# Expert-choice feed-forward on one core: first output unit reordered, weight sums and list tables moved

## Chip, core and metric

The kernel runs on one core of one Trainium2 chip. The metric is the device time of one execution in microseconds (us). TensorE (PE) multiplies, VectorE (DVE) and ScalarE (ACT) do the elementwise work, GpSimd (POOL) and SyncE (SP) issue transfers. Each engine works through its own queue in order, and semaphores tie the queues together.

## What is computed

The reference, cut to what matters (8 x 512 tokens of 512 values, 8 experts, 1024 tokens for each, 2048 hidden values):

```python
y = clip(einsum('blc,oc->blo', x * styles, weight) * dcoefs + bias, -256, 256)
scores = softmax(y @ Wr)                      # over 8 experts
G, idx = top_k(scores.T, 1024)                # each expert takes its best tokens
h = gelu(einsum('ekd,edh->ekh', y[idx], W1) + b1)
X_e = einsum('ekh,ehd->ekd', h, W2) + b2
out = x + zeros.at[idx].add(G[..., None] * X_e)
```

## The kernel before, in words

All products are in fp32. A first part (to about 130 us) forms y and the scores, stores both in a table in device memory, and finds expert 0's token list: `route_first` gives the position of each token as two digits, `first_indices` (L909 to L942) turns the digits into one-hot tables `hot` (L918), `val` (L923, L924) and `oh` (L930), and 64 small products `ps_idx` give the list. Fillers (`idle`) keep TensorE going beside it. `first_tokens` then gathers the tokens.

The rest is 16 pairs of a hidden and an output stage: for each expert `e` two halves `p` of the hidden values. Each product of a stage is done as a 2 x 2 block product with seven products instead of eight: p1 = a11 b11, p2 = a12 b21, p3 = s4 b22, p4 = a22 t4, p5 = s1 t1, p6 = s2 t2, p7 = s3 t3. The s are sums of blocks of the left side (`left_sums`, L978 to L983, on VectorE, in the order s3, s1, s2, s4), the t sums of the weights' blocks. t1 and t3 of w2 are made by accumulating transfers that POOL issues (L205, L206); t2 and t4 are two additions on VectorE (L221, L222, 128x1024).

*Hidden stage* (`hidden_stage`): the seven products are split into seven again (`second_level`), and a written list `ORDER` says in which order all of them go; "2b6" is inner step 6 of outer product 2 for half b. At a letter "w" other work is put in: the list `work` that the caller hands over, by place 0 to 3. The place of w2's sums is U - 2 = 2, the third "w", between 2b2 and 1b1. Results leave the accumulation banks (PSUM) by ScalarE copies (L1129) and VectorE additions (L1138 after step 2, L1149 after 5, L1157 after 4), and `hidden_outputs` adds them up (L1196, L1212 to L1216) and applies gelu on ScalarE (L1197).

*Output stage*: four units `out_unit`, one for each 128 rows of both token halves. `in_turns` runs them: it takes the first five steps of a unit as its own and keeps the other two as `held`, which it runs inside the next unit, one after that unit's first step and one after its second. Unit v: p1, p2, p6, p7, p5, then p3 and p4 held. Steps p1, p6, p5, p3 add up in one bank of tag a, and ScalarE copies the partial sum (`snap_o`, L1328) between them; p2 has tag b (one bank), p7 and p4 share one of two banks of tag c. A finished half row goes out by an indirect transfer that adds to the result (`send`, L1361).

The scheduler of the language may move instructions within what the dependencies allow; the order it makes on each engine is part of the build, and a reader sees it in the trace. Tile tags with a fixed number of buffers (`bufs`) decide what waits for what.

Of the kernel before, what the change touches and what calls it, by code (L numbers as in the profile page):

```python
# [12 lines left out]
BF16 = mybir.dt.bfloat16  # L13
I32 = mybir.dt.int32
AF = mybir.ActivationFunctionType
ALU = mybir.AluOpType
# [4 lines left out]
P = 128  # L21
# [4 lines left out]
def tile_modulated_expert_choice_ffn(  # L26
# [15 lines left out]
    nc = tc.nc  # L42
    B, L, C = x.shape
    W = condT.shape[0]
    E, D, H = w1.shape
    N = B * L
    K = max(4, math.ceil(N * 2.0 / E))
    NT = N // P
# [4 lines left out]
    GH = HALF // P  # L53
# [5 lines left out]
    YW = D + E  # L59
# [8 lines left out]
    wpool = ctx.enter_context(tc.tile_pool(name="weights", bufs=1))  # L68
# [6 lines left out]
    behind = {}  # L75
# [18 lines left out]
    ps = ps_mm.tile([P, HALF], F32, tag="c", name="ps_idle0", bufs=2)  # L94
# [817 lines left out]
    def first_indices():  # L912


        lo, hi = places[0]
        hot = gp.tile([P, 2 * GH * YW], BF16, tag="xg", name="hot_0")[:, 0 : NT * HI].rearrange(
            "p (t h) -> p t h", h=HI)
        nc.vector.tensor_tensor(hot, hi.unsqueeze(2).to_broadcast([P, NT, HI]),  # L918
                                iota_hi.unsqueeze(1).to_broadcast([P, NT, HI]), ALU.is_equal)
        both = gp.tile([P, 2 * GH * YW], BF16, tag="xg", name="oh_0")  # L920
        val = both[:, 0 : 2 * NT * HI].rearrange("p (t a h) -> p t a h", a=2, h=HI)
        oh = both[:, 2 * NT * HI : 2 * NT * HI + NT * LO].rearrange("p (t m) -> p t m", m=LO)
        nc.scalar.mul(val[:, :, 0, :], hot, iota_p[:, 0:1])  # L923
        nc.vector.tensor_tensor(val[:, :, 1, :], hot,  # L924
                                iota_t.unsqueeze(2).to_broadcast([P, NT, HI]), ALU.mult)
        parts = 4
        ps = ps_small.tile([P, 2, KG], F32, tag="small", name="ps_idx0")
        for n in range(parts):
            here = slice(n * NT // parts, (n + 1) * NT // parts)
            nc.vector.tensor_tensor(  # L930
                oh[:, here, :], lo[:, here].unsqueeze(2).to_broadcast([P, NT // parts, LO]),
                iota_lo[:, 0:LO].unsqueeze(1).to_broadcast([P, NT // parts, LO]), ALU.is_equal)
            for t in range(NT)[here]:
                for q in range(P // LO):
                    in_order(partial(
                        nc.tensor.matmul, ps[q * LO : (q + 1) * LO, :, :], oh[:, t, :],
                        val[:, t, :, :].rearrange("p a (g q) -> p q a g", q=P // LO)[:, q, :, :],
                        start=(t == 0), stop=(t == NT - 1), skip_group_check=True))
        idle(IDLE2, ps_mm.tile([P, HALF], F32, tag="b", name="ps_idle2"))
        idx_f = rt2.tile([P, KG], F32, tag="idx_f", name="idx_f_0")  # L940
        nc.vector.tensor_reduce(idx_f, ps.rearrange("p a k -> p k a"), AX.X, ALU.add)
        nc.vector.tensor_copy(idx[:, 0, :], idx_f)  # L942
# [120 lines left out]
    def bank(tag, name, bufs):  # L1063
        return ps_mm.tile([P, HALF], F32, tag=tag, name=f"ps_{tag}_{name}", bufs=bufs)

    def in_turns(units, between, keep=False, behind={}):

        held = []
        nxt = units[0]()
        for n in range(len(units)):
            unit = nxt
            if n + 1 < len(units):
                nxt = units[n + 1]()
            first = unit[:5]
            first[0]()
            if held:
                held[0]()  # L1080
            mark = first[1]()
            if held:
                held[1]()
            for f in first[2:]:
                mark = f() or mark
            for work in between.get(n, ()):
                with tc.issue_after(behind.get("last", mark).ins):
                    work()
            held = unit[5:]
        if keep:  # L1090
            return held
        for f in held:
            f()
# [211 lines left out]
    def out_unit(e, p, v, H, b2_sb):  # L1305

        _, gain, ngain = tokens[e]
        blk = w2_blocks[e, p]
        name = f"o{e}_{p}_{v}"
        c = v * P  # L1310
        a = {(i, k): H[:, :, k, i * HALF + c : i * HALF + c + P] for i in range(2) for k in range(2)}
        s = {n: sp.tile([P, HALF], F32, tag=f"snap{t}", name=f"h{n}_{name}").rearrange(
            "p (k m) -> p k m", m=P) for n, t in (("s2", 1), ("s3", 2), ("s4", 4))}
        s["s1"] = a[1, 0]
        with tc.issue_after(summed["last"].ins) if v == 1 else ExitStack():
            summed["last"] = left_sums(a[0, 0], a[0, 1], a[1, 0], a[1, 1], s)
        s["11"], s["12"], s["22"] = a[0, 0], a[0, 1], a[1, 1]
        G = [(gain[:, g : g + 1], ngain[:, g : g + 1]) for g in (v, v + GH)]
        o = [op.tile([P, D], F32, tag=f"o{i}", name=f"o{i}_{name}", bufs=2 + i) for i in range(2)]
        st = {}  # L1320

        def mm(ps, left, right, start):
            product(ps, [s[left][:, k, :] for k in range(U)],
                    [blk[right][:, k, :] for k in range(U)], start)

        def snap(n, scale):
            t = sp.tile([P, QD], F32, tag=f"osnap{n}", name=f"snap{n}_{name}", bufs=SNAPS[n])
            nc.scalar.mul(t, st["a"], scale)  # L1328
            return t

        def p1():
            st["a"] = bank("a", name, 2)[:, 0:QD]
            mm(st["a"], "11", (0, 0), True)
            st["s1"] = snap(1, G[0][0])

        def p2():
            b = bank("b", name, 1)[:, 0:QD]
            mm(b, "12", (1, 0), True)
            return nc.vector.scalar_tensor_tensor(o[0][:, 0:QD], b, G[0][0], st["s1"],
                                                  op0=ALU.mult, op1=ALU.add)  # L1340

        def p6():
            mm(st["a"], "s2", "t2", False)
            st["u2"] = snap(2, G[1][0])

        def p7():
            st["c"] = bank("c", name, 2)[:, 0:QD]
            mm(st["c"], "s3", "t3", True)

        def p5():  # L1350
            mm(st["a"], "s1", "t1", False)
            st["u4"] = snap(4, G[1][1])
            nc.vector.scalar_tensor_tensor(o[1][:, QD:D], st["c"], G[1][1], st["u4"],
                                           op0=ALU.mult, op1=ALU.add)

        def send(i):
            if p == 0:
                nc.vector.scalar_tensor_tensor(o[i], b2_sb, G[i][0], o[i],  # L1358
                                               op0=ALU.mult, op1=ALU.add)
            g = i * GH + v  # L1360
            sent["last"] = nc.gpsimd.indirect_dma_start(  # L1361
                out=last_rows[g] if e == E - 1 else out_rows,
                out_offset=bass.IndirectOffsetOnAxis(ap=idx[:, e, g : g + 1], axis=0),
                in_=o[i][:, :], in_offset=None, compute_op=ALU.add,
            )

        def p3():
            mm(st["a"], "s4", (1, 1), False)
            nc.scalar.mul(o[0][:, QD:D], st["a"], G[0][1])
            send(0)  # L1370

        def p4():
            mm(st["c"], "22", "t4", False)
            nc.vector.scalar_tensor_tensor(o[1][:, 0:QD], st["c"], G[1][0], st["u2"],
                                           op0=ALU.mult, op1=ALU.add)
            send(1)

        def last_p7():
            p7()
            nc.vector.scalar_tensor_tensor(o[1][:, 0:QD], st["c"], G[1][0], st["u2"],  # L1380
                                           op0=ALU.mult, op1=ALU.add)

        def last_p4():
            b = bank("b", name + "_p4", 1)[:, 0:QD]
            mm(b, "22", "t4", True)
            nc.vector.scalar_tensor_tensor(o[1][:, 0:QD], b, G[1][0], o[1][:, 0:QD],  # L1386
                                           op0=ALU.mult, op1=ALU.add)
            send(1)

        if (e, p, v) == (E - 1, NP - 1, GH - 1):  # L1390
            return [p1, p2, p6, last_p7, p5, last_p4, p3]
        return [p1, p2, p6, p7, p5, p3, p4]
# [16 lines left out]
    for e in range(E):  # L1409
# [3 lines left out]
        for p in range(NP):  # L1413
            nxt = (e, p + 1) if p + 1 < NP else (e + 1, 0)
            if e or p:
                H = fx.tile([P, U, 2, KG * P], F32, tag="H", name=f"H_{e}_{p}")
            work = {U - 2: [partial(sums, "w2", w2_blocks, (e, p))]}
            if e == p == 0:
                work[0] = [route_others]
            if p == NP - 1 and e + 1 < E:  # L1420
# [15 lines left out]
            if e == p == 0:  # L1436
                work[0] = [partial(second_sums, 0)]
            held = in_turns([partial(out_unit, e, p, v, H, b2_sb) for v in range(GH)], work,
                            keep=nxt[0] < E, behind=summed)


# [38 lines left out]
```

## Time and profile before

| what | value |
|---|---|
| median of 3 runs | 1663.96 us (1662.77 to 1664.11) |
| profiled execution | 1666.56 us, its span 1664.8 us |
| mean granted TensorE clock | 0.995 |
| hidden stage, expert 0 second half (273 to 325 us) | TensorE busy 52.0, VectorE 44.6, ScalarE 31.3 us |
| output stage, expert 0 second half (325 to 364 us) | TensorE busy 39.0, VectorE 38.8, ScalarE 6.2 us |
| sums of w2, L221 and L222 | 16 of each, median 1219 and 1218 ns |

A line of the timeline gives the start in us from the span's start, the length, the engine, the line of the kernel, the operation, what is written and read, the shape and the number of instructions merged; in brackets is the idle time before it and who ended it. A 128x256 matmul in fp32 is recorded as two instructions ("x8" is one product of a unit). The ends of matmuls are modelled, so two in a row overlap in the records, and only their starts tell of a short pause.

### The profile page before, as it was taken

How to read it: one execution, taken by the hardware profiler on the slowest of the kernel's cores; microseconds unless marked ns; L12 is line 12 of the kernel's file. 1: busy time of each engine (PE TensorE's matmuls, PEld its weight loads, DVE VectorE, ACT ScalarE, POOL GpSimd, SP SyncE). 2: the span in 40 equal slices, each digit the busy share in tenths (PEclk: the TensorE clock that was granted, in tenths of full speed). 3: DMA queues.
4: the chain of work that ended last, by engine and by line, in shares of the span. 5: the costliest groups of instructions: out<-in, count | busy, mean ns of one | idle time of the engine just before them, and what ended most of it. 6: DMA issues, size and time to landing. Idle time of an engine off the chain costs nothing. (4 is left out here: it accounts for less than half of the span.)

```text
span 1664.8 us, 22093 instructions
## 1 busy us (share of the span) xinstructions
PE 1637.1 (98%) x8001; PEld 1376.2 (83%) x8001; DVE 1309.3 (79%) x2392; ACT 665.0 (40%) x1505; POOL 432.7 (26%) x296
## 2 busy tenths in 40 slices
PE   9998999999999999999999999999999999999998
PEld 5785568888888888888888888888888888888887
DVE  5885699888879786978789686978689786977681
ACT  3543322516152533525161534435261625344351
POOL 0111004231342214230434224230423134331302
PEclk9999999999999999999999999999999999999999
DMA  9724716872686546963686557873686358774604
GB/s 210 187 52 151 237 51 126 211 155 49 128 207 149 120 102 140 238 122 79 116 190 151 95 108 165 210 133 85 120 202 151 59 125 187 171 133 102 127 1 51
DMA packets 178461, 224.51 MB, mean 135 GB/s; under 512 B 18216, under 2 KB 117288, under 8 KB 178224
## 3 DMA queue, kind: packets, MB, share of 16 engines
q0 software_dynamic: 48368, 92.69, 32.8%
q1 hardware_dynamic: 129968, 130.40, 27.9%
q8 instruction: 63, 1.03, 0.3%
q14 instruction: 46, 0.38, 0.1%
q10 hardware_dynamic: 16, 0.02, 0.0%
HBM read 166.07 MB, written 65.37 MB: 139 GB/s over the span
## 5 line engine op out<-in xcount | busy, mean ns | idle before, releaser
L1361 POOL DMA_INDIRECT out<-o_o,idx x128 | 265.5, 2074 | 601.2 <-DVE o_o L1358 80.6
L1129 ACT ACTIVATE q<-ps_qa 128x256 f32<-128x256 f32 x450 | 168.9, 383 | 145.9 <-PE ps_qa L1098 101.2
L1328 ACT ACTIVATE snap_o<-ps_a_o,gain 128x256 f32<-128x256 f32 x128 | 60.5, 473 | 337.6 <-PE ps_a_o L1098 337.6
L1196 DVE TENSOR_TENSOR H<-H,q 128x512 f32<-128x512 f32 x240 | 159.9, 687 | 22.2 <-ACT H L1153 12.0
L1197 ACT ACTIVATE H<-H,b_sb 128x512 f32<-128x512 f32 x240 | 166.1, 717 | 27.1 <-DVE H L1196 23.9
L1098 PE MATMUL ps_c_qc<-x_sums,w_l 128*128 128x256 f32 x420 | 126.6, 383 | 1.4 <-DVE H L1157 1.4
L1098 PE MATMUL ps_a_o<-w,H 128*128 128x256 f32 x512 | 127.0, 380 | 0.0
L1098 PE MATMUL ps_c_qc<-x_l,w_sums 128*128 128x256 f32 x420 | 125.1, 379 | 0.9 <-DVE H L1149 0.9
L1098 PE MATMUL ps_c_o<-w,hs_o 128*128 128x256 f32 x512 | 125.3, 382 | 0.0
L1098 PE MATMUL ps_b_qb<-x_l,w_l 128*128 128x256 f32 x420 | 125.0, 379 | 0.0
L1098 PE MATMUL ps_b_o<-w,H 128*128 128x256 f32 x512 | 123.7, 379 | 0.0
L1098 PE MATMUL ps_a_o<-w_t,hs_o 128*128 128x256 f32 x512 | 122.3, 381 | 0.0
L1098 PE MATMUL ps_a_o<-w,hs_o 128*128 128x256 f32 x512 | 121.2, 379 | 0.0
L1098 PE MATMUL ps_a_o<-w_t,H 128*128 128x256 f32 x512 | 121.2, 379 | 0.0
L206 POOL DMA_DIRECT2D w_l<-in_w x14 | 18.4, 1313 | 388.8 <-DMA w_l<-in_w 207.8
L1098 PE MATMUL ps_c_o<-w_t,H 128*128 128x256 f32 x504 | 119.1, 379 | 0.0
L1098 PEld LDWEIGHTS ps_c_o<-w,hs_o 128*128 128x128 f32 x512 | 95.9, 190 | 18.3 <-DVE hs_o L980 5.4
L1098 PEld LDWEIGHTS ps_a_o<-w_t,hs_o 128*128 128x128 f32 x512 | 96.0, 190 | 15.9 <-issue 3.4
L1098 PEld LDWEIGHTS ps_a_o<-w_t,H 128*128 128x128 f32 x512 | 96.4, 190 | 14.4 <-issue 0.5
L1098 PEld LDWEIGHTS ps_a_o<-w,H 128*128 128x128 f32 x512 | 96.6, 190 | 13.9 <-issue 1.1
L1098 PEld LDWEIGHTS ps_b_o<-w,H 128*128 128x128 f32 x512 | 97.1, 190 | 13.2
L1098 PEld LDWEIGHTS ps_a_o<-w,hs_o 128*128 128x128 f32 x512 | 95.6, 190 | 14.8
(326 smaller groups left out, 3289.2 us busy)
## 6 DMA issues: line engine op xcount, KB each, us to landing
w_l<-in_w SPq DMA_DIRECT2D x70, 512.0 KB
w<-in_w SPq DMA_DIRECT2D x64, 512.0 KB
rows<-xg SPq DMA_DIRECT2D x56, 260.0 KB
xg<-rows SPq DMA_DIRECT2D x56, 256.0 KB
w_l<-in_w POOLq DMA_DIRECT2D x28, 512.0 KB
w_t<-in_w SPq DMA_DIRECT2D x15, 512.0 KB
w<-in_w POOLq DMA_DIRECT2D x15, 512.0 KB
w_t<-in_w POOLq DMA_DIRECT2D x15, 512.0 KB
```

The source lines that it names most:

```text
L206: nc.gpsimd.dma_start(out=out[0, 1], in_=where[1, 1], accum_op=ALU.add)
L1098: nc.tensor.matmul(ps, lefts[k], rights[k], start=(start and k == 0), stop=(k == n - 1), skip_group_check=True)
L1129: nc.scalar.mul(t, st["a"], scale)
L1196: nc.vector.tensor_add(out[i, j], out[i, j], st[n])
L1197: nc.scalar.activation(out[i, j], out[i, j], AF.Gelu, bias=bias[j], scale=scale)
L1328: nc.scalar.mul(t, st["a"], scale)
L1361: sent["last"] = nc.gpsimd.indirect_dma_start(out=last_rows[g] if e == E - 1 else out_rows, out_offset=bass.IndirectOffsetOnAxis(ap=idx[:, ...
```

## The change

Three edits.

1. In each output stage the unit v = 0 gets another list of steps: p1, p2, p4, p7, p6, p5, p3, where p4 has a bank of tag c of its own, ScalarE copies its product to the output row, and the other parts are added to that row as they come. The list of five own steps so ends with p6, and p5 and p3 are held. `in_turns` gets `ahead`: the second unit's p1 is then run right after the first unit's p4.
2. The sums of w2 go to place U - 1 = 3, the fourth "w", between 6b2 and 5b1, in all stages but expert 0's first half.
3. `hot`, `val` and `oh` of `first_indices` lie in the tiles `w2_t2` and `w2_t4` of the weights' pool instead of the gather pool's tag "xg".

```diff
-        hot = gp.tile([P, 2 * GH * YW], BF16, tag="xg", name="hot_0")[:, 0 : NT * HI].rearrange(
-            "p (t h) -> p t h", h=HI)
+        room, oh = [wpool.tile([P, 2 * U * QD], BF16, tag=f"w2_t{n}", name=f"digits_{n}")
+                    for n in (2, 4)]
+        hot = room[:, 0 : NT * HI].rearrange("p (t h) -> p t h", h=HI)
...
-        both = gp.tile([P, 2 * GH * YW], BF16, tag="xg", name="oh_0")
-        val = both[:, 0 : 2 * NT * HI].rearrange("p (t a h) -> p t a h", a=2, h=HI)
-        oh = both[:, 2 * NT * HI : 2 * NT * HI + NT * LO].rearrange("p (t m) -> p t m", m=LO)
+        val = room[:, NT * HI : 3 * NT * HI].rearrange("p (t a h) -> p t a h", a=2, h=HI)
+        oh = oh[:, 0 : NT * LO].rearrange("p (t m) -> p t m", m=LO)
...
-    def in_turns(units, between, keep=False, behind={}):
+    def in_turns(units, between, keep=False, behind={}, ahead=False):
...
             first = unit[:5]
-            first[0]()
+            if not begun:
+                first[0]()
+            begun = False
...
-            for f in first[2:]:
+            for k, f in enumerate(first[2:]):
                 mark = f() or mark
+                if ahead and n == k == 0:
+                    nxt[0]()
+                    begun = True
...
+        def first_p4():
+            ps = bank("c", name + "_p4", 2)[:, 0:QD]
+            mm(ps, "22", "t4", True)
+            nc.scalar.mul(o[1][:, 0:QD], ps, G[1][0])
+        def first_p7():
+            p7()
+            nc.vector.scalar_tensor_tensor(o[1][:, 0:QD], st["c"], G[1][0], o[1][:, 0:QD],
+                                           op0=ALU.mult, op1=ALU.add)
+        def first_p6():
+            p6()
+            nc.vector.tensor_add(o[1][:, 0:QD], o[1][:, 0:QD], st["u2"])
+        def first_p5():
+            p5()
+            send(1)
+        if v == 0:
+            return [p1, p2, first_p4, first_p7, first_p6, first_p5, p3]
...
-            work = {U - 2: [partial(sums, "w2", w2_blocks, (e, p))]}
+            work = {(U - 1 if e or p else U - 2): [partial(sums, "w2", w2_blocks, (e, p))]}
...
-                            keep=nxt[0] < E, behind=summed)
+                            keep=nxt[0] < E, behind=summed, ahead=True)
```

## Prediction

> **What bounds the kernel now.** I read the page first, then who TensorE waits for, then the order in time of single stages. The page says that TensorE is busy nearly throughout (at a mean granted clock of 0.995):
>
> ```profile
> PE 1637.1 (98%) x8001; PEld 1376.2 (83%) x8001; DVE 1309.3 (79%) x2392; ACT 665.0 (40%) x1505; POOL 432.7 (26%) x296
> ```
>
> So only TensorE's pauses can be won. The list of waits names few (line, releaser, total, times, longest):
>
> ```profile
> PE ps_idx L81 <- DVE oh L924: 3.9, 1, 3.9
> ...
> PE ps_c_qc L1098 <- DVE H L1157: 1.4, 2, 0.8
> ```
>
> It hides pauses shorter than a matmul's modelled tail, so I compare starts. Eight 128x256 matmuls in a row start 1.73 us after the last eight: 0.216 us each. Where an output stage begins (expert 1, first half):
>
> ```profile
> 415.64 1.46 PE L1098 MATMUL ps_a_o<-w,H 128*128 128x256 f32 x6
> 417.03 1.56 PE L1098 MATMUL ps_c_o<-w,hs_o 128*128 128x256 f32 x6
> 418.45 1.97 PE L1098 MATMUL ps_a_o<-w_t,hs_o 128*128 128x256 f32 x8
> 420.26 0.59 PE L1098 MATMUL ps_c_o<-w,hs_o 128*128 128x256 f32 x2
> ```
>
> From 415.64 to 420.26 are 4.62 us for 20 matmuls, which need 4.32: 0.30 us are lost, because `hs_o` comes late from VectorE:
>
> ```profile
> 416.30 0.68 DVE L980 TENSOR_TENSOR hs_o<-H 128x512 f32<-128x512 f32 x1
> 417.01 0.69 DVE L981 TENSOR_TENSOR H<-H 128x512 f32<-128x512 f32 x1
> 417.62 0.68 DVE L982 SCALAR_TENSOR_TENSOR hs_o<-hs_o,H 128x512 f32<-128x512 f32 x1
> ```
>
> The second pause lies in the hidden stage before, where the two sums of w2 stand ahead of L1157, which frees a bank of tag c:
>
> ```profile
> 392.46 1.22 DVE L221 TENSOR_TENSOR w_t<-w_t,w 128x1024 f32<-128x1024 f32 x1
> 393.60 0.42 DVE L1149 TENSOR_TENSOR H<-q,ps_c_qc 128x256 f32<-128x256 f32 x1
> 393.94 1.22 DVE L222 TENSOR_TENSOR w_t<-w_t,w 128x1024 f32<-128x1024 f32 x1
> 395.07 0.42 DVE L1157 TENSOR_TENSOR H<-ps_c_qc,q 128x256 f32<-128x256 f32 x1
> ```
>
> ```profile
> 394.95 0.59 PE L1098 MATMUL ps_c_qc<-x_l,w_sums 128*128 128x256 f32 x2
> 395.54 0.70 PE L1098 MATMUL ps_c_qc<-x_sums,w_l 128*128 128x256 f32 x2
> ...
> 397.84 0.70 PE L1098 MATMUL ps_a_qa<-x_sums,w_l 128*128 128x256 f32 x2
> 398.37 0.59 PE L1098 MATMUL ps_c_qc<-x_sums,w_l 128*128 128x256 f32 x2
> ```
>
> From 394.95 to 398.37 are 14 matmuls: 3.42 us against 3.02, so 0.40 us lost. Both pauses recur in each of 15 stages (all but expert 0's first half). Twice the sums also waited for their weights, and TensorE with them:
>
> ```profile
> 945.59 1.23 DVE L221 TENSOR_TENSOR w_t<-w_t,w 128x1024 f32<-128x1024 f32 x1 [1.83 <-DMA w_t<-in_w]
> ```
>
> After it TensorE took 3.47 us (945.74 to 949.21) for 6 matmuls worth 1.30; at 1500 the wait for L1157 was 0.81 us where 0.16 is usual. Beyond the ordinary 0.40 the two lost 1.90 and 0.65: 2.55 us.
>
> **Part 1, the order of the first output unit.** No matmul is added. Now p4 (H22 with w2's t4) comes third and the second unit's p1 fourth: sixteen matmuls, 3.45 us, that need no `hs_o`. p7, which began at 417.03 waiting, would begin at 415.64 + 3.45 = 419.09; its `hs_o` of L980 was ready at 416.98. p6 begins at 420.8, and L982 was done at 418.30. The 0.30 us go: 15 x 0.30 = 4.5 us. p4 itself needs H22 (its product 7 of the second level comes before 3 and 4 in the written order, and p2 already waits for 3) and t4, made some 15 us earlier.
>
> What could be late next is p5. It adds to the bank that p6's copy on ScalarE still reads, and p7 no longer lies between. The built order puts half of the second unit's p2 there: four matmuls, 0.86 us. The same arrangement stands today between p5 and p3: the last matmul of p5 starts about 422.63, its copy runs 423.05 to 423.52, and p3 starts at 423.71 without a pause. So 0.1 to 0.2 us remain and I take nothing; without the cover it would be 0.7 us a stage. ScalarE's copy of p4 (0.47 us by the same rows) and of the second p1 are over before p6 ends. Bounds: 0 to 0.25 us a stage.
>
> Added: one copy on ScalarE, and on VectorE one more operation of 128x256 (three in place of two, 0.35 to 0.42 us each), 16 times. ScalarE is 6.2 us busy in the 39 us of an output stage. VectorE is full in the second halves (38.8 of 39 us), so there everything behind shifts by up to 0.8 us; but the last sum of w1 ended at 548.57 and its first user on TensorE came at 552.34. The 3.8 us cover it; uncovered it would be 8 x 0.4 = 3 us. On POOL the two scatters of the first unit change places, so the first waits for p5's result instead of p3's; SP's queue keeps its order, and POOL passes no load. The accumulating w2 load behind them (463.6 in the next stage) has tens of us. Nothing.
>
> **Part 2, the sums of w2 one place later.** In the built order L221 now follows the L1138 of product 6b2, eight operations on, about 5 us. There VectorE was idle 0.46 and 0.42 us between operations (397.8, 399.0), and it arrives with no backlog, while at 392.46 it had none to spare since 387. But the situation is alike: counted from 6b2's start, it ends at 0.59; L1138 at 0.63, L221 at 0.96, an H sum at 2.1, L222 at 2.7, L1149 at 3.85, L1157 from 4.18 to 4.6. The c product that needs this L1149 is due ten products on, at 4.32 (its release comes at 4.3), the one that needs this L1157 at 4.75. So the bank pause is about gone. L1157 also frees the copy buffer of ScalarE's next `q`; that copy would end at 5.2, and its product is due at 5.18: 0.05 late and 0.1 to restart. I take 0.15 us left of 0.40, 15 x 0.25 = 3.75 us; bounds 0 (all remains) and 6.0, and below nothing if VectorE comes late there. The late weights get 5 us more, against 1.83 missed: 2.55 us gone in this execution.
>
> The page "Perfetto Trace Analysis", section "Optimization Strategy", speaks against this part: a gap that keeps recurring can mean too few SBUF or PSUM buffers. By it the hidden stage, which gets no bank, keeps its 0.40 us, and part 2 yields only 2.55. The rows say that the bank is there but that L222 stands in front of the operation that frees it, so I go with the rows and keep the rule's number as a rival.
>
> **Part 3, the tables.** They leave the pool whose space the last `ytok` transfer still holds:
>
> ```profile
> 154.30 0.69 DVE L918 TENSOR_TENSOR hot<-hi,iota_hi 128x512 bf16<-128x512 bf16 x1 [1.21 <-DMA y_dram<-ytok]
> ...
> 156.29 2.35 PE L81 MATMUL ps_idx<-oh 128*64 128x16 bf16 x64 [3.95 <-DVE oh L924]
> ```
>
> `hi` was done at 153.1. Now a piece of `oh` goes first (0.6 us), `hot` at 153.75 instead of 154.30, and the chain starts 0.6 us sooner, up to 1.2 if a later wait shrinks too. "TensorE: Matmul & The Clock Gate", section "What's actually happening", lets the clock fall to half after an idle window of some 3.4 us. Shortening 3.9 us to 3.3 would by that rule keep the clock. The trace grants 0.50 from 154.62 to 161.44, so the window that counts ended before either start; and the matmuls after it are fillers that wait for the gather. By the rule some 1.5 us more, by the row nothing; I take 0.6, bounds 0 and 2.5.
>
> **Sum.** 4.5 + 3.75 + 2.55 + 0.6 = 11.4 us from the profiled execution's 1666.56 (span 1664.8): 1655.2. The median of the runs, 1663.96, is 2.6 us lower; the late weights may be part of that, so against it I count them at half: 4.5 + 3.75 + 1.3 + 0.6 = 10.1, hence **1654 us**.
>
> **Rivals.**
> *The sums only move their pause* (the rule above): 4.5 + 1.3 + 0.6 = 6.4, 1657.5 us. For it: the same two sums of 1.15 us between the same kind of products. Against: no backlog in front. Chance 0.24.
> *p5 waits for p6's copy* 0.25 us in each stage, which eats most of part 1: 10.1 - 3.75 = 6.3, also 1657.5 us. For it: the cover is 0.1 to 0.2 us. Against: p5 and p3 do this today. Chance 0.11.
> *All pauses go and the start gains its clock*: 4.5 + 6.0 + 2.55 + 2.0 = 15, 1649 us. Chance 0.11.
> *Slower:* in the fourth place both sums stand ahead of three releases (b, c, copy buffer), and ScalarE, in order, waits behind them. If L221 starts 0.65 us later than I reckon, the copy's product waits 0.8 us and 15 x 0.4 = 6 us are lost against today, which cancels the 6.4; at 1.1 us more than today it is 15 x 0.7 = 10.5 lost, 1668 us. Against: VectorE is idle just before. Chance 0.06.
> That the order doesn't change is excluded: it is in the build. The pauses' going without moving the time, because the weights' transfers become the bound, would give about 1663: chance 0.06.
> The main case keeps 0.42.
>
> **Numbers.** About 0.2% (3.3 us) can be told from no change, so "faster" is below 1660.6. Main case, the two weaker gains and the large gain lie there (0.88; of it 0.05 may fall short): 0.83. Same 0.10, slower 0.07. Range 1649 to 1661.
>
> **What would show it.** Right: at each output stage, p7's first matmul 3.45 us after p4's with no excess over 0.216 us, p5 0.86 us after p6's end, and no row of TensorE waiting for L1149 or L1157 (now L1156, L1164) of 0.8 us; `hot` with no DMA ahead of it. Wrong: a wait of p5 for a `snap_o` copy, `ps_a_qa` or `ps_qa` waiting for `q` longer than 0.1 us behind L222, or an L221 that still waits for DMA.

## Result and profile after

| | before | after |
|---|---|---|
| median of 5 runs | 1663.96 us (1662.77 to 1667.16) | 1673.94 us (1672.67 to 1675.47) |
| profiled execution, its span | 1666.56, 1664.8 us | 1672.67, 1670.9 us |
| mean granted TensorE clock | 0.995 | 0.997 |

The ratio is 1.0051 (95% interval 1.0041 to 1.0062): the change costs some 8 us by the ratio, 10 by the medians of the table, where a gain of 10 was predicted. In the new kernel the lines from L914 to L1060 lie 1 or 2 lower, those of `out_unit` 7 lower: L1339 is now L1346, L1353 is L1360, L1361 is L1368, L1369 is L1376, L1149 and L1157 are L1156 and L1164.

The page of the kernel after: TensorE looks no busier or idler than before, but one of its groups has idle time of its own (last column: idle time ahead of it, and who ended that).

```profile
PE 1632.4 (98%) x8001; PEld 1376.4 (82%) x8001; DVE 1313.4 (79%) x2408; ACT 673.3 (40%) x1521; POOL 445.7 (27%) x296
...
L1105 PE MATMUL ps_b_o<-w,H 128*128 128x256 f32 x512 | 124.3, 380 | 9.1 <-DVE o_o L1346 9.1
```

The list of waits of the kernel after (total, times, longest). None of these rows exists in the list of before:

```profile
DVE o_o L1346 <- DMA out<-o_o,idx: 38.0, 8, 4.9
...
ACT o_o L1376 <- DMA out<-o_o,idx: 13.5, 7, 2.1
...
PE ps_b_o L1105 <- DVE o_o L1346: 9.1, 7, 1.5
...
PE ps_c_o L1105 <- DVE o_o L1360: 4.3, 8, 0.6
```

It reads from top to bottom: a VectorE operation that writes the output row `o_o` waits for a transfer out of `o_o` that is still reading; TensorE waits for that operation, because it also empties bank b. TensorE's rows for L1149 and L1157 and VectorE's for `w_t` and `hot` are gone.

**What was forecast to go has gone.** Timeline of TensorE, kernel after, expert 1's first half, where the output stage begins:

```profile
417.26 1.89 PE L1105 MATMUL ps_c_o_p<-w_t,H 128*128 128x256 f32 x8
...
420.72 1.89 PE L1105 MATMUL ps_c_o<-w,hs_o 128*128 128x256 f32 x8
422.44 1.89 PE L1105 MATMUL ps_a_o<-w_t,hs_o 128*128 128x256 f32 x8
```

p7 starts 3.46 us after p4 and is not broken into pieces any more; no time is lost. The two sums of w2 in their new place, VectorE and then TensorE, kernel after, the hidden stage ahead of it:

```profile
399.52 1.22 DVE L221 TENSOR_TENSOR w_t<-w_t,w 128x1024 f32<-128x1024 f32 x1
...
401.26 1.22 DVE L222 TENSOR_TENSOR w_t<-w_t,w 128x1024 f32<-128x1024 f32 x1
```

```profile
402.87 0.69 PE L1105 MATMUL ps_c_qc<-x_l,w_sums 128*128 128x256 f32 x2
403.39 0.59 PE L1105 MATMUL ps_c_qc<-x_sums,w_l 128*128 128x256 f32 x2
403.83 0.65 PE L1105 MATMUL ps_qa<-x_l,w_sums 128*128 128x256 f32 x2
404.31 0.59 PE L1105 MATMUL ps_a_qa<-x_sums,w_sums 128*128 128x256 f32 x2
```

From 402.87 to 404.31 are 1.44 us for six matmuls worth 1.30: 0.14 us are left of 0.40. And the tables, kernel after:

```profile
153.67 0.68 DVE L920 TENSOR_TENSOR digits<-hi,iota_hi 128x512 bf16<-128x512 bf16 x1
...
155.61 1.81 PE L81 MATMUL ps_idx<-digits,digits 128*64 128x16 bf16 x64 [3.25 <-DVE digits L925]
```

**What came instead.** Seven of the eight waits for L1346 lie in the output stages of the second halves, the eighth in expert 0's first half, where `second_sums` stand at the same place. In the last second half, which prepares no tokens, and in the other first halves `o1` is first too and nobody waits. POOL's timeline in expert 1's second half, before and after (start, length of the issue, idle time before it and who ended it):

```profile
518.77 1.64 POOL L1361 DMA_INDIRECT out<-o_o,idx  x1 [0.57 <-ACT o_o L1369]
526.86 1.57 POOL L1361 DMA_INDIRECT out<-o_o,idx  x1 [6.45 <-DVE o_o L1374]
```

```profile
527.45 1.81 POOL L1368 DMA_INDIRECT out<-o_o,idx  x1 [7.65 <-DVE o_o L1360]
532.99 6.51 POOL L1368 DMA_INDIRECT out<-o_o,idx  x1 [3.73 <-DMA out<-o_o,idx]
```

Before, the first unit's `o0` left first, as soon as ScalarE had p3 (518.77), and `o1` followed. After, `o1` leaves first, and p5's operation (L1353 before, L1360 after), which now completes it, stands behind `prepare` of the next expert's tokens (it begins with L1020) in VectorE's queue. Before, then after, with ScalarE's L1376, which completes `o0`, between:

```profile
516.75 0.44 DVE L1353 SCALAR_TENSOR_TENSOR o_o<-ps_c_o,ngain,snap_o 128x256 f32<-128x256 f32 x1
```

```profile
515.49 2.36 DVE L1020 STREAM_TRANSPOSE x_l<-xg 128x1024 f32<-128x1024 f32 x2
...
521.42 0.47 ACT L1376 ACTIVATE o_o<-ps_a_o,ngain 128x256 f32<-128x256 f32 x1 [2.12 <-PE ps_a_o L1105]
...
526.68 0.48 DVE L1360 SCALAR_TENSOR_TENSOR o_o<-ps_c_o,ngain,snap_o 128x256 f32<-128x256 f32 x1
```

`o0`, complete at 521.9, stands behind `o1` on POOL, where the second transfer waits for the landing of the first (3.73 us in the row). It goes at 532.99, 14.2 us later than before. `o0` has two buffers, so the third unit's L1346 writes where the first unit's row lies; it also empties the one bank b, which the fourth unit's p2 needs. VectorE and TensorE, kernel after:

```profile
543.00 0.48 DVE L1346 SCALAR_TENSOR_TENSOR o_o<-ps_b_o,gain,snap_o 128x256 f32<-128x256 f32 x1 [4.92 <-DMA out<-o_o,idx]
```

```profile
540.21 1.89 PE L1105 MATMUL ps_a_o<-w,hs_o 128*128 128x256 f32 x8
543.54 1.99 PE L1105 MATMUL ps_b_o<-w,H 128*128 128x256 f32 x8 [1.44 <-DVE o_o L1346]
```

The fourth unit's p2 was due at 541.94 and starts at 543.54, 1.6 us late; p4 behind it loses 0.8 us more.

To compare runs I add up, over each whole trace, by how much the start of each matmul came later than the usual distance for its shape, and sort this by place and releaser (us). "Routing" is the small products that make the other experts' token lists. Span minus this sum is 1608 to 1610 us in every trace, so the pauses account for the differences between the spans to within about 1.5 us.

| trace | span | to 182 us | routing | left sums and rest | bank c, late weights | behind `o_o` |
|---|---|---|---|---|---|---|
| before | 1664.8 | 36.0 | 3.0 | 6.9 | 9.1 | 0 |
| before, again | 1660.9 | 32.5 | 3.0 | 6.9 | 9.1 | 0 |
| after | 1670.9 | 34.2 | 3.6 | 2.7 | 3.0 | 18.7 |
| after, o0 first | 1651.2 | 33.5 | 3.7 | 2.7 | 2.9 | 0 |
| first edit alone | 1676.2 | 33.6 | 3.6 | 2.7 | 6.7 | 19.9 |
| first edit alone, o0 first | 1666.8 | 39.0 | 3.8 | 2.7 | 12.1 | 0 |
| the same again | 1660.4 | 31.5 | 3.6 | 2.7 | 12.9 | 0 |
| second edit alone | 1660.7 | 38.0 | 3.0 | 7.0 | 2.8 | 0 |
| third edit alone | 1666.8 | 34.9 | 3.0 | 6.9 | 13.1 | 0 |
| second and third | 1656.0 | 34.3 | 3.0 | 6.9 | 2.9 | 0 |

The first 182 us differ by some 8 us between traces without regard to the edits, so single spans tell little; the columns to the right of it tell more.

### The profile page after: what moved, and what is told of

Same layout as the page of the kernel before. It is cut to its first block, busy times and chain, and to the rows that moved or that the text cites. A ratio compares the mean times of both kernels' runs of the same rounds, so it can differ in the third digit from the quotient of the medians.

```text
span 1670.9 us, 22124 instructions
## 1 busy us (share of the span) xinstructions
PE 1632.4 (98%) x8001; PEld 1376.4 (82%) x8001; DVE 1313.4 (79%) x2408; ACT 673.3 (40%) x1521; POOL 445.7 (27%) x296
## 4 chain that ended last, share of the span: by engine, by line
PE 74%; DMA 10%; DVE 10%; issue 2%; ACT 2%; SPq 1%; POOL 0%; another core or an unknown queue 0%; POOLq 0%; DVEq 0%; ACTq 0%
PE ps_a_o L1105 16%; PE ps_qa L1105 15%; PE ps_c_qc L1105 10%; PE ps_c_o L1105 8%; DMA out<-o_o,idx 7%; PE ps_a_qa L1105 6%; PE ps_b_qb L1105 5%; PE ps_b_o L1105 3%; DMA w_l<-in_w 2%; PE ps_ya L81 2%; PE ps_yc L81 1%; PE ps_y L81 1%; PE ps_c_o_p L1105 1%; ACT xmT L544 1%; PE ps_a_h L1105 1%
## 5 line engine op out<-in xcount | busy, mean ns | idle before, releaser
L1368 POOL DMA_INDIRECT out<-o_o,idx x128 | 280.5, 2191 | 619.6 <-DVE o_o L1360 118.2
L1203 DVE TENSOR_TENSOR H<-H,q 128x512 f32<-128x512 f32 x240 | 160.9, 686 | 17.5 <-ACT H L1160 12.1
L1105 PE MATMUL ps_c_o<-w,hs_o 128*128 128x256 f32 x512 | 121.0, 379 | 0.0
L1335 ACT ACTIVATE snap_o<-ps_a_o,ngain 128x256 f32<-128x256 f32 x64 | 30.4, 474 | 179.1 <-PE ps_a_o L1105 147.2
```

The source lines that it names most:

```text
L1105: nc.tensor.matmul(ps, lefts[k], rights[k], start=(start and k == 0), stop=(k == n - 1), skip_group_check=True)
L1203: nc.vector.tensor_add(out[i, j], out[i, j], st[n])
L1368: sent["last"] = nc.gpsimd.indirect_dma_start(out=last_rows[g] if e == E - 1 else out_rows, out_offset=bass.IndirectOffsetOnAxis(ap=idx[:, ...
```

## Experiments

*Scatter theory*: `o1` first, and finished late, lets `o0` leave late; its occupied buffer holds up L1346, and L1346 holds up bank b. *VectorE rival*: the operation that was added for the first unit makes a full VectorE late by itself, and the transfers only follow. *Other edits*: the loss is the second's or the third's. Every kernel below computes all of the reference.

**o0 first.** The kernel after, with

```diff
         def first_p5():
             p5()
-            send(1)
+        def first_p3():
+            p3()
+            send(1)
...
-            return [p1, p2, first_p4, first_p7, first_p6, first_p5, p3]
+            return [p1, p2, first_p4, first_p7, first_p6, first_p5, first_p3]
```

> The changed kernel, but the first unit sends its row o0 ahead of o1 again (both after p3); nothing else moves. Scatter theory: in the second halves o0's transfer waits on POOL behind o1's, and o1 waits for L1360, which VectorE reaches late; unit 2 writes into the same o0 buffer (two copies) and so frees bank b late. With o0 sent first its landing comes some 14 us sooner, L1346 waits for no transfer, and the 8 waits of about 2.3 us go: 1674 - 18.4 = 1655.5 us (1653 to 1658). VectorE rival: the operation that was added to a full VectorE queue makes L1346 and L1360 late by itself, the transfers only follow: 1672 to 1674, and the waits of TensorE for L1346 stay near 1.5 us.

1651.19 us, ratio to before 0.9929 (0.9907 to 0.9950). TensorE waits for no operation on `o_o` any more (of VectorE's eight waits for a landing one is left, 0.9 us), with every VectorE operation still there. That ends the VectorE rival. POOL in this kernel:

```profile
516.72 2.01 POOL L1368 DMA_INDIRECT out<-o_o,idx  x1 [1.18 <-ACT o_o L1376]
524.27 9.76 POOL L1368 DMA_INDIRECT out<-o_o,idx  x1 [5.55 <-DMA out<-o_o,idx]
```

`o0` goes at 516.72. `o1` now has the very slow issue, 9.76 us, and nobody waits for it: `o1` has three buffers.

**Three buffers for o0, two for o1** (`bufs=2 + i` becomes `bufs=3 - i`):

> The changed kernel with three buffers for o0 and two for o1 instead of two and three (three and three don't fit); the order of the transfers stays as in the changed kernel. Scatter theory: unit 2's o0 has a buffer of its own, the late landing holds nobody, and the waits of TensorE for L1346 go: 1655.5 us (1653 to 1658), unless o1 with two buffers makes a wait of its own, which would show as an L1360 or a ScalarE copy that waits for a transfer. VectorE rival: 1672 to 1674. A rival by which the order of the transfers itself is what costs (POOL held, or the memory): also 1674, though the run with o0 first is fast.

1695.02 us, ratio 1.0187 (1.0164 to 1.0210): slower than the kernel after. The waits for L1346 are gone, as forecast, and the exception that the forecast named has come, in the same place, 8 times, for `o1`. VectorE:

```profile
556.44 0.48 DVE L1360 SCALAR_TENSOR_TENSOR o_o<-ps_c_o,ngain,snap_o 128x256 f32<-128x256 f32 x1 [6.29 <-DMA out<-o_o,idx]
```

So a buffer that stays occupied is the link, whichever tile is short. Three of each, the clean cure, does not fit into the memory and wasn't tried.

**The first edit alone** (second and third taken back):

> The kernel before with the first edit alone (order of the first unit). If the loss is the first edit's, and the others give what was forecast (3.75 + 1.3 + 0.6 us): 1674 + 5.7 = 1679.5 us (1676 to 1682), with 8 waits for L1346 of about 2.3 us in all. If the loss comes from the second or third edit: 1659.5 (1664 - 4.5).

1677.72 us, ratio 1.0080 (1.0060 to 1.0101), as forecast. The whole loss, 19.9 us in the table, is the first edit's.

**Only the two transfers swapped, in the kernel before** (p3 of unit 0 doesn't send; p4 sends 1, then 0):

> The kernel before with one thing changed: the first unit's two transfers change places on POOL (o1 first, then o0, both after p4). No matmul moves and no operation is added. Scatter theory: o1's transfer starts at about 526.9 in expert 1's second half, o0's at about 532.3 instead of 518.8 and lands near 542; unit 2's L1339 waits for it from 536.5, and TensorE's p2 of unit 3, at 541.1 before, comes some 1.5 to 2 us late, 8 times: 1664 + 12 to 16 = 1676 to 1680 us. VectorE rival (the added operation is the cause): 1664, no difference.

1747.81 us, ratio 1.0494 (1.0469 to 1.0518). The mechanism appears without any matmul moved, against the VectorE rival; its size is far above what I had reckoned. POOL shows why:

```profile
538.24 11.14 POOL L1361 DMA_INDIRECT out<-o_o,idx  x1 [8.55 <-DVE o_o L1375]
553.35 1.54 POOL L1361 DMA_INDIRECT out<-o_o,idx  x1 [3.97 <-DMA out<-o_o,idx]
```

The issue of `o1` takes 11.14 us instead of 1.6, so `o0` starts at 553. TensorE waits 6.1 to 6.4 us seven times for L1339, and up to 2.6 us for L1353 in the first halves too.

**The token work one place later** (o1 first as in the kernel after; `prepare` stands with `second_sums` behind the second unit):

```diff
-                work[0] = [partial(prepare, e + 1)]
-                work[1] = [partial(second_sums, e + 1)]
+                work[1] = [partial(prepare, e + 1), partial(second_sums, e + 1)]
```

> The changed kernel, o1 still sent ahead of o0, but the next expert's token work on VectorE comes in one place later, behind the second unit's steps, so that the first unit's L1360 stands ahead of it. Scatter theory, sharpened: o1 first costs only because o1 is finished late. L1360 then runs near 521.5 instead of 526.7 in expert 1's second half, o0's transfer starts near 527 and lands near 537, ahead of L1346's turn: the 8 waits shrink from 2.3 us to below 0.5, some 1656 to 1660 us. If the order of the transfers costs however early o1 is done: 1672 to 1674. The shift can make waits of its own (the second unit's L1360, the token sums that the next hidden stage needs); those would show under other lines.

Ratio 0.9998 (0.9988 to 1.0007), 1667.86 us beside 1668.4 for before on that chip. POOL starts `o1` at 520.40 and `o0` at 526.83, and TensorE's waits for L1346 fall to 0.21 us: `o1` first costs little when `o1` is done early. The time forecast was missed by 0.2 to 0.4%, because the shift makes waits of its own, L1360 1.3 to 1.5 us in three stages (9.1 us behind `o_o` in this trace, where the kernel after has 18.7).

**What sets the size.** In the kernel after, `o0` also took 6.51 us to be issued, while VectorE worked without a break. This run moves the four 2.0 us token sums away (`second_sums` goes to place 2) and leaves all else:

> The changed kernel (o1 first, o1 late as there), but the sums of the next expert's tokens (four operations of 2.0 us on VectorE) go one place later, behind the third unit's steps. In the changed kernel the issue of o0's transfer on POOL starts at 533.0 and takes 6.5 us where 1.55 is usual, while VectorE works without a break on those sums; it lands at 542.9. If that stretch decides the size of the wait, o0's issue now takes 1.6 to 3 us and it lands near 538 to 539.5, ahead of TensorE's turn at 541.5: the 8 waits for L1346 fall from 1.5 us (start to start) below 0.3. If the late start alone decides, they stay near 1.5. The sums themselves come some 3 us later and may make the next hidden stage wait under other lines (x_sums, w_sums, q), so the total is open: 1656 (no new wait) to 1680.

1684.21 us, ratio 1.0115 (1.0089 to 1.0141), more than the 1680 at which the range ended. POOL, then TensorE:

```profile
527.35 1.81 POOL L1368 DMA_INDIRECT out<-o_o,idx  x1 [7.56 <-DVE o_o L1360]
533.16 1.71 POOL L1368 DMA_INDIRECT out<-o_o,idx  x1 [4.01 <-DMA out<-o_o,idx]
```

```profile
541.83 1.89 PE L1105 MATMUL ps_b_o<-w,H 128*128 128x256 f32 x8
546.56 2.68 PE L1105 MATMUL ps_c_o<-w_t,H 128*128 128x256 f32 x8 [2.84 <-DVE o_o L1360]
```

`o0` starts at the same time (533.16 beside 532.99), is issued in 1.71 us, and the wait for L1346 is gone from TensorE (541.83, on time). So the late start alone would still have been covered; the stretched issue decided. But VectorE still idles 4.8 us at L1346, and the moved sums then stand ahead of the next L1360: a wait of 3.0 us in the place of 2.3, and behind most of these waits the clock falls (last section), hence slower.

**The parts one by one.** The first edit alone with o0 first:

> The kernel before with the first edit alone, but with the first unit's o0 sent ahead of o1. This takes the disputed cost away and leaves the term forecast for the order of products, 15 x 0.30 = 4.5 us: 1663.6 - 4.5 = 1659.1 us. If p5's copy or the added VectorE operation cost anything, less: up to 1663. If the order gives more than was reckoned (all of the 12.4 us that the version with o0 first gained in all would be 4.5 + 7.9 for the other edits): 1657.

The second edit alone:

> The kernel before with the second edit alone (sums of w2 in the fourth place). Forecast: 3.75 us for the bank pause and 1.3 for late weights: 1658.5 us, TensorE's waits for L1164 of 0.15 us a stage. If the sums only move their pause: 1662.3. If the pause goes wholly (15 x 0.40): 1656.3.

The third alone:

> The kernel before with the third edit alone (list tables in other tiles). Forecast: 0.6 us, 1663.0; bounds 1663.6 (nothing) and 1661.1 (the whole start gains its clock).

Ratios on one chip, in this order (before: 1668.4): 1.0005 (0.9994 to 1.0016), 0.9955 (0.9943 to 0.9968), 0.9996 (0.9986 to 1.0006). The sums gave 7.5 us (5.3 to 9.5), more than the 5.05 forecast (3.75 + 1.3), and the tables nothing that can be told apart. The order gave nothing where 4.5 us were forecast, although its pause is gone from the trace (6.9 to 2.7): bank c and late weights took 12.1 in place of 9.1. To see whether that is chance, four kernels together on another chip:

> The kernel before itself, to have its trace and its time from the same chip as the next three; ratio 1. If the late weights are a matter of the chip or of chance, its L221 waits for weights a few times here too (2 in the first trace), and the pauses at L1149 and L1157 sum to between 8 and 13 us.

> The changed kernel without its first edit (sums and tables only). From the traces: bank pauses 8.8 to 2.8 us and the table's pause 4.1 to 3.4: 6.0 + 0.7 = 6.7 us less than before, ratio 0.996; more (8 to 10 us) where the weights come late in the kernel before. If the first edit were needed for the gain: nothing.

> The first edit alone with o0 sent first, again, now beside a trace of the kernel before from the same chip. Its trace had the pause for the left sums gone (3.2 us in all) and the pauses for late weights larger by 3.1 us. If these are chance: ratio 0.998 here (2.5 to 3.2 us less), as many late weights as the kernel before. If the order itself makes the weights late (the output stage ends sooner, so that the next weights have less time): ratio 1.000 again, and more late weights than in the kernel before.

> The changed kernel with o0 sent first, again, beside the version without the first edit. If the first edit gives its 2.5 to 3.2 us once the sums come later: 2.5 to 3.2 us less than the version with sums and tables only, about 10 us less than before (ratio 0.994). If its order gives nothing whatever goes beside it: the same time as that version.

Before itself: 1.0004 (0.9992 to 1.0016). Second and third edit: 1654.74 us, 0.9955 (0.9942 to 0.9968). First edit with o0 first: 1662.91, 1.0001 (0.9991 to 1.0010). All three with o0 first: 1652.04, 0.9940 (0.9927 to 0.9953). The order gave nothing alone, both times, and 2.7 us beside the sums (1654.74 - 1652.04; the intervals of the two ratios overlap a little, so the size is loose). In both traces of it alone L221 waited 5 times for weights, 4.6 and 5.2 us; in two traces of before 3 and 2 times, 2.1 and 2.4 us. The third edit alone, with the old order, had 4 waits and 6.0 us; the first edit alone with `o1` first, whose output stages run longer, had none. So late weights eat what the order gains as long as the sums stand early; whether the order itself makes them late or only meets them isn't settled.

The kernel with o0 first is the fastest of all that were measured, and faster than before on both chips.

## Why the prediction was wrong, point by point

- *Part 1, POOL: "the first waits for p5's result instead of p3's ... Nothing."* This is the step that failed. It asked which loads POOL passes, and saw only that `o1` would be first; it didn't ask when p5's result leaves VectorE, nor who waits for the landing of `o0`. The page and the code had both: VectorE full for 38.8 of 39 us, p5 moved behind `prepare`, and two buffers for `o0`. Nor did it ask how long an issue takes while VectorE works on its sums (6.51 us where 1.6 is usual). What the runs showed in place of "nothing": 18.7 us in the trace. With o0 first they are gone: 1651 and 1652 us (ratios 0.9929 and 0.9940), where 1654 (0.9940) was predicted for a change without this cost. That these meet is in part luck: of the terms, the order gave 2.7 us for 4.5, the sums 7.5 for 5.05, the tables nothing visible for 0.6.
- *Part 1, the pause for the left sums, 4.5 us*: right in the trace, too large as a gain. The timeline of before has 0.30 us in each of the 15 stages, after none. 0.7 us came back at the routing products, which the sum didn't have. Net it was worth 2.7 us beside the other edits and nothing alone.
- *Part 1, p5 behind p6's copy*: right, no such wait in any trace.
- *Part 1, the added VectorE operation covered*: right; with o0 first it is there and TensorE waits for nothing behind it.
- *Part 2*: right in mechanism and size. 0.14 us are left in the stage shown (0.15 forecast), L221 waits for no weights, and bank c falls by 6.1 to 6.3 us (3.75 + 2.55 = 6.3 forecast). That they were to count half against the median was too careful: the runs gave 7.5. The rival that the sums only move their pause is out.
- *Part 3*: right in the trace. `hot` waits for no transfer, the pause ahead of `ps_idx` fell from 3.95 to 3.25 us (0.6 forecast, 0.7 measured); too little to be seen in the times. The further gain from the clock, which the rule in the prediction would have given for a pause of 3.3 us, did not come: the clock is 0.50 after it too (155.8 to 162.6 us; before 154.6 to 161.4), as the prediction's row had it.
- *The rivals*: the slower one (the sums late in their fourth place) didn't happen. None of the rivals had the output row's two buffers in it.

## What to carry to other kernels

When two results change places in an in-order queue of transfers, follow both ends: when the new first one is really finished on its own engine's queue, and which later writer needs the buffer of the one that now goes second. A transfer that is late is waited for where its row has no spare buffer; count buffers against the distance in units before calling a swap free. If a forecast gain is visible in the trace and the time still rises, put the old order back in the one queue and leave the rest, as was done here for some 20 us (ratio 1.0051 to 0.9929).

## What the hardware showed that I had not expected

**In these traces an indirect transfer's issue on POOL waits for a break in VectorE's work on SBUF** (the memory that holds the tiles). Of the 128 transfers of `o_o` in the kernel after, the 24 that met no VectorE operation between SBUF tiles took 1.54 us (median, 1.62 at most). The one at 532.99 came when such an operation had just begun; they follow each other without a break until 538.08, and the issue ends at 539.50, 1.42 us later. With o0 first, the one at 524.27 met a chain until 532.62, where L1346 reads PSUM; it ends at 534.03, 1.41 us later. All 78 issues of over 5 us in the fifteen traces end 1.4 to 1.5 us behind such a break. A transfer that gets in first isn't held up: the one at 526.86 in the kernel before took 1.57 us although a 2.0 us addition began 0.03 us after it (0.01 us ahead was not enough for the one at 538.24 in the run with the transfers swapped). The Trainium skill's page "SBUF — State Buffer", section "SBUF: two separate sides", describes it: VectorE and GpSimd share a port pair that one of them holds alone, and a transfer that GpSimd issues can't have its descriptors written meanwhile. Its trap is told of VectorE's fast copies, and operations with two SBUF inputs are said to clash only with a GpSimd operation that reads SBUF; here additions of two fp32 tiles did it, and several in a row without a break let nothing in. In the kernel before, the first unit's `o0` had the quiet duration (1.64 us at 518.77), so its row showed none of this. But the same trace has two issues of `o1` that took 10.47 us (at 895.00) and 11.05 us (at 1447.52) and that nobody waited for: the price of an issue behind VectorE's sums could be read before the change.

**Behind most pauses of near 3 us TensorE's clock fell to half.** In the run with the token sums later, TensorE pauses seven times for 2.7 to 3.0 us (start to start, above the usual distance) at L1360. Behind six of these the granted clock is 0.50 for 3.4 us, beginning 0.2 to 1.2 us after TensorE has started again; the one of 2.73 us was spared. With the transfers swapped in the kernel before, it fell behind four of six pauses of 2.5 to 2.8 us. In the kernel after, pauses of up to 1.6 us leave it at 1.00. A window of the run with the token sums later (PE busy, weight load, VectorE, ScalarE, POOL, granted clock, DMA share, GB/s):

```profile
548.00:549.50 1.50, 1.50 (x5) 1.12 (x5) 1.50 (x1) 0.00 (x0) 1.04 (x1) 0.50 0.00 0
```

The matmul distance there goes from 0.216 to 0.426 us for about eight matmuls. So this pause of 3.0 us (2.84 in the records) costs 8 x 0.21 = 1.7 us more behind it: a wait twice as long as that of the kernel after costs more than twice as much. What decides between the pauses that cost the clock and those that don't isn't shown by their length alone.
